# Eight attention layers on one core: where the keys' first halves stand in the queues, and which engine normalizes the first tile behind the output's product

## The chip, the core and the metric

The kernel runs on one core of a Trainium2 chip. A core has five engines with queues of their own: TensorE (PE in the profile; its weight loads are PEld), VectorE (DVE), ScalarE (ACT), GpSimd (POOL) and SyncE (SP), which here only starts DMAs. ScalarE starts DMAs too; such an instruction stands in ScalarE's queue like any other. An engine takes its instructions in order, and one that waits for another engine's result holds up all that are queued behind it. SBUF is the memory that all engines work on, PSUM the memory that TensorE writes its products to.

The metric is the device time of one execution in microseconds (us). A profiled execution also gives its span, from the first instruction to the last.

## What is computed

The reference is a Perceiver block of three stages on 512 tokens with 512 features, all in float32: a cross attention over 8192 context rows, eight layers of linear attention with a feed-forward part, and a stage of experts. The change is in the eight layers. Cut to that stage:

```python
def _block(x, p):
    Wq, bq, Wk, bk, Wv, bv, Wo, bo, ln1_s, ln1_b, Wf1, bf1, Wf2, bf2, ln2_s, ln2_b = p
    residual = x
    q = jnp.einsum('nld,da->nla', x, Wq) + bq
    k = jnp.einsum('nld,da->nla', x, Wk) + bk
    v = jnp.einsum('nld,da->nla', x, Wv) + bv
    Q = jax.nn.elu(q) + 1.0
    K = jax.nn.elu(k) + 1.0
    KV = jnp.einsum('nsh,nsh->nh', K, v)
    Ksum = jnp.sum(K, axis=1)
    Z = 1.0 / (Q * Ksum[:, None, :] + EPS_Z)
    V = Q * KV[:, None, :] * Z
    attn = jax.nn.gelu(jnp.einsum('nla,ad->nld', V, Wo) + bo)
    x = _layernorm(attn + residual, ln1_s, ln1_b)
    residual = x
    h = jax.nn.gelu(jnp.einsum('nld,df->nlf', x, Wf1) + bf1)
    ff = jax.nn.gelu(jnp.einsum('nlf,fd->nld', h, Wf2) + bf2)
    x = _layernorm(ff + residual, ln2_s, ln2_b)
    return (x, None)
```

## The kernel before, in words

**Tiles.** The 512 tokens are four tiles of 128 (t = 0 to 3), the 512 features four chunks of 128. A tensor named `cur` or `mid` has tokens on the partitions; `curT` and `midT` are the same, transposed, with features on the partitions. Weight matrices (1 MB each) come through SyncE's DMA queue into eight buffers. Six rows of biases and scales (`row`, 256 KB each) come for each layer through ScalarE's queue (L985) into nine buffers in rotation, so that a load of a coming layer waits until the last reader of an older row is done. The second and third row of layer l + 1 take the buffers of two rows that GpSimd reads at the end of layer l - 1 (L936 and L937, the affine step of the two last tiles), and ScalarE's queue has these two loads at the start of layer l. Layer 7 has no next layer to load rows for.

**Order of the work.** TensorE's order is written out by hand. For the other engines a scheduler chooses the order from the program's dependences and its own estimates; `tc.issue_after(x)` tells it that what is inside may stand in its queue only behind x.

**The features of a layer** (`features`, L638). TensorE first makes the halves of the keys for the tokens of tiles 0 and 1 (`k7.p12`), the queries' first products for the same tokens, then turns tile 2 (`turns[2]()`: four transposes into PSUM, and four copies of ScalarE into `curT`, L945), makes a third query product, turns tile 3, and makes the products of tiles 2 and 3 and then the rest of the keys by a seven-product scheme (`k7.rest`), for which sums of the two halves of the tokens are needed (`token_sums`, L719 to L722, on VectorE and GpSimd). In layer 0 the turning is `transpose_into` (L594, L595).

`k7.take` (L744) takes the first two of the keys' products out of PSUM: a copy by ScalarE (L747), an addition by VectorE (L748), and then `elu1`: L623 on VectorE, L625 and L626 on ScalarE (L626 is an exponential, with a load of the activation table ahead of it), L627 on GpSimd and L628 on VectorE. Before the change it is told to stand behind the turned copies of tile 2, and behind the last normalization of the layer before (`normed`).

**Behind the output's product** (L1063 to L1072). For each tile, TensorE multiplies by the output's weights (L1069) and `finish` (L913) adds the bias (L917, VectorE), takes the GELU (L918, ScalarE), adds the residual (L919, VectorE) and normalizes: statistics (L922, L923), an inverse square root by nine small VectorE operations (L91 to L95, L82), and the scaling. With `eng` ScalarE the scaling is two instructions, a small VectorE one (L931) and ScalarE's (L932); with `eng` VectorE it is one (L928). The scaled tile 0 is turned in the midst of tile 3's product, tiles 1, 2 and 3 later, between the products of the hidden features (`s7.p12`, L726). `turn` is four transposes (L943) and four ScalarE copies into `midT` (L945).

Of the kernel before, what the change touches and what calls it, by code (L numbers as in the profile page):

```python
# [11 lines left out]
ALU = mybir.AluOpType  # L12
# [4 lines left out]
P = 128  # L17
D = 512
DC = D // P
# [26 lines left out]
R_BO, R_S1, R_B1, R_BF2, R_S2, R_B2 = range(6)  # L46
# [8 lines left out]
def perceiver_kernel(  # L55
# [3 lines left out]
    nc = tc.nc  # L59
# [28 lines left out]
    def rsqrt_of(var, n, eps, eng=nc.vector):  # L88

        ve = small.tile([P, n], F32, tag=f"ve{n}", name="ve")  # L90
        eng.tensor_scalar(ve, var, eps, None, ALU.add)  # L91
        vh = small.tile([P, n], F32, tag=f"vh{n}", name="vh")
        eng.tensor_scalar(vh, ve, -0.5, None, ALU.mult)
        yg = small.tile([P, n], I32, tag=f"yg{n}", name="yg")
        eng.tensor_scalar(yg, ve.bitcast(I32), -0.5, float(0x5F3759DF), ALU.mult, ALU.add)  # L95
        y = yg.bitcast(F32)
        for _ in range(3):
            t = small.tile([P, n], F32, tag=f"nt{n}", name="nt")
            if n == 1:
                stt(eng, t, y, y, vh, ALU.mult, ALU.mult)  # L100
            else:
                eng.tensor_tensor(t, y, y, ALU.mult)
                eng.tensor_tensor(t, t, vh, ALU.mult)
            y2 = small.tile([P, n], F32, tag=f"ny{n}", name="ny")
            latest[0] = stt(eng, y2, t, 1.5, y, ALU.add, ALU.mult)
            y = y2
        return y
# [10 lines left out]
    def normalize(dst, src, n, eps, roots=None):  # L118
        mv, r = roots or (moments(src, n), None)
        if r is None:  # L120
            r = rsqrt_of(mv[:, :, 1], n, eps)
        for i in range(n):
            last = nc.vector.tensor_scalar(
                dst[:, i, :], src[:, i, :], mv[:, i, 0:1], r[:, i : i + 1], ALU.subtract, ALU.mult
            )
        return last
# [38 lines left out]
    behind, copied, newest = [None, None], [None], [None, None]  # L165
# [46 lines left out]
    k_sb, v_sb, xT, part, rows_of, trigs = {}, {}, {}, {}, {}, {}  # L212
# [118 lines left out]
    while min(met) < NCHUNK:  # L331
        p = k % NPAIR
# [33 lines left out]
    scores, mx, mrow, alpha, mbc, es, po = {}, {}, {}, {}, {}, {}, {}  # L366
# [158 lines left out]
    last = -1  # L525
    for u, n in enumerate(size):
# [6 lines left out]
        for i in range(n):  # L533
            d = end[u] + 1 + i * span // n // 2
            at(d, late_exponentials if d in end[-3:] else exponentials, u, i)
            last = max(d + 1, first)
# [53 lines left out]
    def transpose_into(dst, src, t, space, tag):  # L590

        pt = space.tile([P, DC, P], F32, tag=tag, name="pt")
        for dc in range(DC):
            nc.tensor.transpose(pt[:, dc, :], src[:, dc * P : (dc + 1) * P], ident)  # L594
        return nc.scalar.copy(dst[:, :, t * P : (t + 1) * P], pt)  # L595

    with ExitStack() as s_:
# [33 lines left out]
        def feature(ps, w, c0, xT, t0=0, n=T):  # L631
            for dc in range(DC):
                nc.tensor.matmul(  # L633
                    ps[:, t0 : t0 + n], w[:, dc, c0 : c0 + P], xT[:, dc, t0 : t0 + n],
                    start=(dc == 0), stop=(dc == DC - 1),
                )

        def features(k7, chunks, xT, turns, done, normed):  # L638

            held = {}

            def product(i, t0=0, n=T):
                if t0 == 0:
                    held[i] = mm.tile([P, T], F32, tag="mm", name="ps")
                feature(held[i], *chunks[i], xT, t0, n)

            if 1 in turns:
                for p in range(2):  # L650
                    k7.p12(p, 0, P, False)
                turns[1]()
                product(0, 0, P)
                for p in range(2):
                    k7.p12(p, P, P, False)
                product(0, P, P)
            else:
                for p in range(2):
                    k7.p12(p, 0, H, False)
                product(0, 0, H)  # L660
            product(1, 0, H)
            turned = turns[2]()
            with tc.issue_after(normed.ins) if normed else nullcontext():
                with tc.issue_after(turned.ins):
                    for p in range(2):
                        k7.take(p)
            product(2, 0, H)
            turned = turns[3]()
            for t in range(2):
                k7.token_sums(t)  # L670
            for t in (2, 3):
                for i in range(2):
                    product(i, t * P, P)
            product(2, H, H)

            with tc.issue_after(turned.ins):
                for i in range(3):
                    done(i, held[i], 0, T)
            k7.rest((0, 1))
            for i in range(3, len(chunks)):  # L680
                product(i)
                done(i, held[i], 0, T)
# [227 lines left out]
                    next_sums(q)  # L910
                return g0, g1

        def finish(ps, old, bias, t, eng, g=None):  # L913

            if g is None:
                g = gpool.tile([P, D], F32, tag="g", name="g")
                nc.vector.tensor_tensor(g, ps, bias, ALU.add)  # L917
            nc.scalar.activation(g, g, AF.Gelu_apprx_tanh)  # L918
            nc.vector.tensor_tensor(g, g, old[:, t, :], ALU.add)  # L919
            mv = small.tile([P, 1, 2], F32, tag="mv1", name="mv")  # L920
            st = small.tile([P, 6], F32, tag="st", name="st")
            nc.vector.bn_stats(st, g)  # L922
            nc.vector.bn_aggr(mv[:, 0, :], st)  # L923
            r = rsqrt_of(mv[:, :, 1], 1, 1e-6)
            if eng is None:
                return g, mv[:, 0, 0:1], r
            if eng is nc.vector:
                last = nc.vector.tensor_scalar(g, g, mv[:, 0, 0:1], r, ALU.subtract, ALU.mult)  # L928
            else:
                n = small.tile([P, 1], F32, tag="nmr1", name="nmr")  # L930
                last = nc.vector.scalar_tensor_tensor(n, mv[:, 0, 0:1], -1.0, r, ALU.mult, ALU.mult)  # L931
                nc.scalar.activation(g, g, AF.Identity, bias=n, scale=r)  # L932
            return g, last
# [27 lines left out]
        cur = cpl.tile([P, TT, D], F32, tag="cur", name="cur0")  # L961
        curT = cpl.tile([P, DC, T], F32, tag="curT", name="curT0")
        last = None
        for t in range(TT):
            with tc.issue_after(last.ins) if t else nullcontext():
                last = normalize(cur[:, t : t + 1], x_sb[:, t : t + 1], 1, 1e-5, rooted.get(t))
        s_.enter_context(tc.manual_schedule(engines={nc.tensor.engine}))
        transpose_into(curT, cur[:, 0, :], 0, acc, "acc")
        turns = {t: lambda dst=curT, src=cur[:, t, :], t=t: transpose_into(dst, src, t, acc, "acc") for t in (1, 2, 3)}
# [9 lines left out]
        for l in range(NL):  # L979
            w_k, w_q, w_v, w_o = ahead if l else first[0]  # L980
            w_1, w_2 = hidden_weights(l) if l else first[1]
            row = []
# [71 lines left out]
            k7 = k7 if l else keys_of_layer(w_k, curT)  # L1054
            k7.sx = [hpool.tile([P, 2, H], F32, tag="h", name="sx") for _ in range(4)]
            k7.tiles, k7.out = keys_tiles, keys_taken
            features(k7, [(w, ac * P) for w in (w_q, w_v) for ac in range(DC)], curT, turns, taken, last if l else None)


            mid = cpl.tile([P, TT, D], F32, tag="cur", name="mid")  # L1060
# [2 lines left out]
            gs = {}  # L1063
            for t in range(TT):
                po = acc.tile([P, D], F32, tag="acc", name=f"po_{l}_{t}")
                for ac in range(DC):
                    if t == TT - 1 and ac == 2:
                        turn(midT, gs[0], 0, *c1)
                    nc.tensor.matmul(  # L1069
                        po, vt[ac][:, t * P : (t + 1) * P], w_o[:, ac, :], start=(ac == 0), stop=(ac == DC - 1)  # L1070
                    )
                gs[t], last = finish(po, cur, row[R_BO], t, nc.scalar)  # L1072
            turns = {t: lambda dst=midT, g=gs[t], t=t, c=c1: turn(dst, g, t, *c) for t in (1, 2, 3)}

            hT = {}
# [52 lines left out]
            for p in range(2, NF // 2):  # L1128
# [13 lines left out]
                last = s7.p4(p)  # L1142
# [20 lines left out]
            cur = cpl.tile([P, TT, D], F32, tag="cur", name="cur")  # L1163
            if l + 1 == NL:
                break
            curT = cpl.tile([P, DC, T], F32, tag="curT", name="curT")
# [8 lines left out]
            for t in (0, 2):  # L1175
                if t:
                    ahead = attention_weights(l + 1)
                g = back.products(t, row[R_BF2], between if t else lambda q: None, next_sums(t))
# [8 lines left out]
            turns = {t: lambda dst=curT, g=gs[t], t=t, c=c2: turn(dst, g, t, *c) for t in (2, 3)}  # L1187
            k7 = made[0]
# [95 lines left out]
        for o in (4, 5):  # L1284
            w = cpl.tile([P, DC, D], F32, tag=("curT", "cur")[o % 2], name=f"f2_{o}")
# [21 lines left out]
        for q in range(1, NSQ):  # L1307
# [9 lines left out]
        po = [  # L1317
            (acc if t < 3 else mm).tile([P, D], F32, tag="acc" if t < 3 else "mm", name=f"po_f{t}")
            for t in range(TT)
        ]  # L1320
# [51 lines left out]
        for o in range(NO + 2):  # L1372
            if o < NO:
                inner(o)
            if o < 2:
                w = weights(big, f2[(6 + o) * 512 : (7 + o) * 512, :], f"f2_{6 + o}", nc.scalar)
# [79 lines left out]
```

## Time and profile before

| | us |
|---|---|
| median of 3 runs (2603.5 to 2603.98) | 2603.82 |
| profiled execution, its own time | 2604.4 |
| its span | 2602.6 |
| start of the output's product (L1069) in layers 0 and 7 | 1281.40, 2414.97 |
| TensorE busy in the span | 2513.4 |
| VectorE, ScalarE, GpSimd busy | 1746.6, 1187.6, 1413.3 |

The layers take up the span from about 1235 to 2510 us; from one layer's output product to the next it is some 162 us. A matmul of float32 shows as two passes of TensorE. The profile's groups give, for a line of the program, how long its instructions kept an engine busy, and how long the engine had been idle before them and for whom. "Idle" there is counted from the modelled end of a pass, which lies about 0.17 us behind the point at which the next pass could have started; times between starts are so much longer. The granted clock is the share of TensorE's full clock that the throttle let through.

### The profile page before, as it was taken

To read this page: it belongs to the slowest core of one execution; us is meant where nothing else is said; L and a number is where in the kernel's file an instruction comes from. 1 tells how busy PE (TensorE), PEld (TensorE's weight loads), DVE (VectorE), ACT (ScalarE), POOL (GpSimd) and SP (SyncE) were. 2 spreads that over 40 slices of the span, in tenths; PEclk is the share of its full clock that TensorE was granted. 3 is DMA by queue.
4 is the path that set the end of the run, shared out by engine and by line. 5 is a ranking of instruction groups with operands and counts; after the bars stand their busy time and mean duration, and the time that the engine had idled before them with its cause. 6 is when DMAs were issued, how large, how long until landed. Compare 5 with 4: busy or idle time off the path is not lost.

```text
span 2602.6 us, 32659 instructions
## 1 busy us (share of the span) xinstructions
PE 2513.4 (97%) x10936; PEld 1513.2 (58%) x10936; DVE 1746.6 (67%) x3762; ACT 1187.6 (46%) x2191; POOL 1413.3 (54%) x1582
## 2 busy tenths in 40 slices
PE   8999999999999999998999999999999999999998
PEld 4434333333343343333687786877868778687763
DVE  4466667767777767885666666666666766667664
ACT  2465556655566666663423415234152341524413
POOL 0255655665566666774356554565545655466512
PEclk9999999999999999998999999999999999999999
DMA  3111011111111111010522232232322323223135
GB/s 135 41 48 48 25 41 41 41 41 41 34 41 42 40 41 41 10 40 17 209 75 95 84 108 79 74 99 80 110 77 73 106 73 110 77 73 98 65 116 193
DMA packets 98376, 187.42 MB, mean 72 GB/s; under 512 B 10336, under 2 KB 10464, under 8 KB 98208
## 3 DMA queue, kind: packets, MB, share of 16 engines
q1 hardware_dynamic: 88496, 167.29, 19.9%
q10 hardware_dynamic: 8688, 15.94, 1.9%
q0 software_dynamic: 1024, 2.10, 0.2%
q8 instruction: 87, 1.43, 0.2%
q14 instruction: 81, 0.66, 0.1%
HBM read 162.22 MB, written 1.05 MB: 63 GB/s over the span
## 4 chain that ended last, share of the span: by engine, by line
PE 71%; DVE 9%; POOL 7%; issue 7%; ACT 5%; DMA 0%; ACTq 0%; SPq 0%; POOLq 0%; DVEq 0%
PE pw L726 11%; PE pb L861 9%; PE ps L633 7%; PE ps L726 7%; PE pv L259 7%; PE pk L230 6%; PE po L455 6%; PE pc L374 6%; DVE sc L434 4%; PE po L1069 4%; ACT sc L377 2%; ACT sc L435 1%; POOL es L445 1%; PE pt L218 1%; PE pf L955 1%
## 5 line engine op out<-in xcount | busy, mean ns | idle before, releaser
L445 POOL TENSOR_TENSOR es<-es,sc 128x1024 f32<-128x1024 f32 x222 | 525.1, 2365 | 114.7 <-ACT sc L435 103.7
L383 DVE TENSOR_TENSOR mx<-pc,mx 128x512 f32<-128x512 f32 x448 | 283.3, 685 | 191.7 <-ACT sc L377 191.5
L435 ACT ACTIVATE sc<-sc 128x1024 f32<-128x1024 f32 x272 | 288.1, 1063 | 243.1 <-DVE sc L434 231.9
L377 ACT COPY sc<-pc 128x512 f32<-128x512 f32 x544 | 284.1, 599 | 92.8 <-PE pc L374 77.4
L434 DVE TENSOR_TENSOR sc<-sc,mbc 128x1024 f32<-128x1024 f32 x272 | 319.4, 1209 | 3.7 <-PE mbc L411 2.2
L374 PE MATMUL pc<-qT,k 64*128 64x512 f32 x1088 | 288.1, 621 | 2.8 <-ACT v L265 1.3
L455 PE MATMUL po<-sc,v 128*64 128x512 f32 x1088 | 265.0, 608 | 0.2 <-DVE mx L383 0.2
L230 PE MATMUL pk<-xn,wkv 128*128 128x512 f32 x544 | 255.1, 613 | 7.1 <-ACT v L265 2.9
L259 PE MATMUL pv<-wkv,xn 128*128 128x512 f32 x544 | 249.6, 602 | 6.2 <-DVE sin L241 3.3
L374 PEld LDWEIGHTS pc<-qT,k 64*128 64x128 f32 x1088 | 101.1, 187 | 183.7 <-issue 78.8
L1080 ACT ACTIVATE h<-h,col 128x256 f32<-128x256 f32 x192 | 103.8, 575 | 220.7 <-DVE h L794 151.0
L230 PEld LDWEIGHTS pk<-xn,wkv 128*128 128x128 f32 x544 | 100.7, 194 | 150.1 <-issue 106.9
L918 ACT ACTIVATE g<-g 128x512 f32<-128x512 f32 x64 | 39.8, 628 | 317.2 <-DVE g L878 218.9
L259 PEld LDWEIGHTS pv<-wkv,xn 128*128 128x128 f32 x544 | 98.6, 190 | 140.5 <-issue 106.6
L726 PE MATMUL pw<-curT,cur 128*128 128x256 f32 (+1 forms) x896 | 177.2, 351 | 0.0
L713 POOL TENSOR_TENSOR cur<-w 128x256 f32<-128x256 f32 x128 | 93.3, 739 | 133.0 <-DVE g L919 83.8
L633 PE MATMUL ps<-curT,wq 128*128 128x128 f32 (+2 forms) x584 | 134.3, 391 | 27.2 <-ACT curT L945 27.0
L726 PEld LDWEIGHTS pw<-curT,cur 128*128 128x128 f32 x896 | 150.4, 191 | 16.7 <-DVE curT L719 0.2
L827 POOL TENSOR_TENSOR sh<-h 128x128 f32<-128x128 f32 x120 | 83.1, 693 | 133.3 <-PE pb L861 128.9
L455 PEld LDWEIGHTS po<-sc,v 128*64 128x64 f32 x1088 | 67.8, 137 | 145.9 <-issue 123.1
L627 POOL TENSOR_SCALAR m<-m 128x512 f32<-128x512 f32 (+1 forms) x80 | 102.0, 1287 | 75.9 <-ACT m L626 75.1
L861 PE MATMUL pb<-tw,sh 128*128 128x256 f32 x540 | 136.3, 380 | 0.0
(252 smaller groups left out, 4649.3 us busy)
## 6 DMA issues: line engine op xcount, KB each, us to landing
w<-in_wf SPq DMA_DIRECT2D x64, 1024.0 KB, 5.3
k<-cos SPq DMA_DIRECT2D x272, 64.0 KB, 2.0
cb<-in_cx SPq DMA_DIRECT2D x62, 256.0 KB, 3.6
row<-in_rows ACTq DMA_DIRECT2D x48, 256.0 KB, 4.6
f<-in_f SPq DMA_DIRECT2D x10, 1024.0 KB, 5.5
tg<-in_trig SPq DMA_DIRECT2D x16, 512.0 KB, 3.8
wk<-in_wk SPq DMA_DIRECT2D x8, 1024.0 KB, 5.2
wq<-in_wq SPq DMA_DIRECT2D x8, 1024.0 KB, 5.2
```

What stands on the lines that cost most here:

```text
L230: nc.tensor.matmul(pk, wkv[:, 0, dc, j * P : (j + 1) * P], xT[b, dc], start=(dc == 0), stop=(dc == DC - 1))
L259: nc.tensor.matmul(pv, xT[b, dc][:, t * P : (t + 1) * P], wkv[:, 1, dc, :], start=(dc == 0), stop=(dc == DC - 1))
L374: nc.tensor.matmul(pc[h], k_sb[b, p][hs, o : o + P], qT[hs, p, :], start=True, stop=True)
L377: copied[0] = nc.scalar.copy(sc[:, h, :], pc[h])
L383: behind[0] = nc.vector.tensor_tensor(mx[u][:, h, :], pc[h], mx[u][:, h, :], ALU.max)
L434: nc.vector.tensor_tensor(sc, sc, mbc[u], ALU.subtract)
L435: nc.scalar.activation(sc, sc, AF.Exp)
L445: nc.gpsimd.tensor_tensor(es[u], es[u], sc, ALU.add)
L455: nc.tensor.matmul(po[u][h * HD : (h + 1) * HD, :], v_sb[b, p][:, t * P + h * HD : t * P + (h + 1) * HD], scores[u, i][:, h, :], start=(i ...
L633: nc.tensor.matmul(ps[:, t0 : t0 + n], w[:, dc, c0 : c0 + P], xT[:, dc, t0 : t0 + n], start=(dc == 0), stop=(dc == DC - 1),)
L726: nc.tensor.matmul(ps, lhs[:, k], rhs[:, k], start=(k == 0), stop=(k == 1))
L861: nc.tensor.matmul(ps[i], lhs, rhs, start=(q == 0 and i in (1, 2, 6, 5, 4)), stop=(q == self.N - 1 and i in (1, 2, 7, 3, 4)),)
```

## The change

In `features` the two calls of `k7.take` move from behind the copies of tile 2 to behind the copies of tile 3, after the sums of the tokens in the program; the wait for the last normalization of the layer before is left out. Behind the output's product, `finish` is told to let VectorE scale tile 0 (the other tiles stay with ScalarE), and to put the residual's addition of tile 1 behind that scaling in VectorE's queue. TensorE's and SyncE's orders stay as they are. The scheduler's orders of VectorE, ScalarE and GpSimd change around the two places.

```diff
-        def features(k7, chunks, xT, turns, done, normed):
+        def features(k7, chunks, xT, turns, done):
...
-            turned = turns[2]()
-            with tc.issue_after(normed.ins) if normed else nullcontext():
-                with tc.issue_after(turned.ins):
-                    for p in range(2):
-                        k7.take(p)
+            turns[2]()
             product(2, 0, H)
             turned = turns[3]()
             for t in range(2):
                 k7.token_sums(t)
+            with tc.issue_after(turned.ins):
+                for p in range(2):
+                    k7.take(p)
...
-        def finish(ps, old, bias, t, eng, g=None):
+        def finish(ps, old, bias, t, eng, g=None, behind=None):
...
             nc.scalar.activation(g, g, AF.Gelu_apprx_tanh)
-            nc.vector.tensor_tensor(g, g, old[:, t, :], ALU.add)
+            with tc.issue_after(behind.ins) if behind else nullcontext():
+                nc.vector.tensor_tensor(g, g, old[:, t, :], ALU.add)
...
-            features(k7, [(w, ac * P) for w in (w_q, w_v) for ac in range(DC)], curT, turns, taken, last if l else None)
+            features(k7, [(w, ac * P) for w in (w_q, w_v) for ac in range(DC)], curT, turns, taken)
...
-                gs[t], last = finish(po, cur, row[R_BO], t, nc.scalar)
+
+                gs[t], last = finish(
+                    po, cur, row[R_BO], t, nc.scalar if t else nc.vector, None, last if t == 1 else None
+                )
```

## The prediction

> **What bounds the kernel now.** I read the page first, then who waited for whom on TensorE over the layers (1235 to 2510 us), then the busy time and granted clock of single stretches of 3.41 us, then the timelines of the two places that the diff touches, in the third layer (layer 2). The page, with the group of the first edit:
>
> ```profile
> PE 2513.4 (97%) x10936; PEld 1513.2 (58%) x10936; DVE 1746.6 (67%) x3762; ACT 1187.6 (46%) x2191; POOL 1413.3 (54%) x1582
> ...
> L633 PE MATMUL ps<-curT,wq 128*128 128x128 f32 (+2 forms) x584 | 134.3, 391 | 27.2 <-ACT curT L945 27.0
> ```
>
> TensorE is busy 97%: only what it waits for can be won. In the layers it has two waits that come back:
>
> ```profile
> PE ps L633 <- ACT curT L945: 27.0, 7, 4.1
> PE pt L943 <- ACT g L932: 5.5, 8, 0.7
> ```
>
> The first comes before the queries' products of the last token tile (layers 1 to 7): six of 4.1 us, and 2.42 in layer 7. The second comes before the first tile's transposes behind the output's product, 0.7 in each of eight layers. The first costs more than its idle time. Columns here: stretch, busy time of PE, PEld, DVE, ACT, POOL, granted clock, DMA:
>
> ```profile
> 1569.43:1572.85 3.42, 0.17 (x2) 0.00 (x0) 2.51 (x4) 2.72 (x5) 2.48 (x4) 1.00 0.22 77
> 1572.85:1576.26 3.41, 2.56 (x12) 2.57 (x13) 2.36 (x7) 2.29 (x7) 2.48 (x3) 0.50 0.33 77
> 1576.26:1579.68 3.42, 3.42 (x12) 2.97 (x12) 0.71 (x2) 3.04 (x6) 1.79 (x2) 0.50 0.00 0
> ...
> 2381.81:2385.22 3.41, 1.36 (x10) 1.26 (x11) 2.47 (x4) 2.82 (x8) 3.41 (x5) 1.00 0.00 0
> 2385.22:2388.63 3.41, 3.41 (x13) 2.96 (x12) 2.64 (x6) 3.32 (x6) 2.17 (x3) 0.50 0.00 0
> ```
>
> After a stretch in which TensorE was mostly idle the clock is 0.50 for the next 3.41 us or two of them. In the chain of waits the work between this wait and the pairs' products took 5.54, 6.66, 5.43, 6.57, 5.41, 6.54 and 5.47 us in layers 1 to 7; at full speed (112 ns a 128-wide pass, 216 a 256-wide one) it is 16 x 0.112 + 8 x 0.216 = 3.52. So 41.6 - 24.6 = 17.0 us are lost beside the 27.0 of idle time.
>
> **First edit: the keys' first halves behind the last tile's copies.** The timeline shows why the copies of tile 3 came late:
>
> ```profile
> 1567.07 0.38 ACT L747 COPY kf<-ps 128x256 f32<-128x256 f32 x1
> 1568.21 1.48 POOL L936 TENSOR_TENSOR cur<-g,row 128x512 f32<-128x512 f32 x1
> 1569.72 0.33 ACTq L985 DMA_DIRECT2D row<-in_rows  x1
> 1569.77 1.32 POOL L937 TENSOR_TENSOR cur<-cur,row 128x512 f32<-128x512 f32 x1
> 1570.88 1.28 ACT L626 ACT_TABLE_LOAD   x1
> 1572.26 0.33 ACTq L985 DMA_DIRECT2D row<-in_rows  x1
> 1573.20 1.48 ACT L945 ACTIVATE curT<-pt,col 128x128 f32<-128x128 f32 x4
> ```
>
> The transposes end at 1567.65 and 16 passes more keep TensorE busy to 1569.44. ScalarE has the keys' copies, activations and a table load ahead of the four copies (1573.20). The edit takes these away, but in ScalarE's new order two row loads (L985) stand between the copies of tile 2 and those of tile 3. They wait for buffers that GpSimd still reads: the first was issued at 1569.72, as L936 ended at 1569.69; the second needs L937, which ends at 1571.09. So it issues at 1571.12, takes 0.33, the copies begin at 1571.45, and the first (0.44, and 0.05 to TensorE as at 1573.64 to 1573.70) lets TensorE on at 1571.95: idle 1571.95 - 1569.44 = 2.5 us by start times in place of 4.26, 2.35 by the page's measure. Layer 7 loads no rows for a next layer, which is why its wait is 2.42 already; there nothing stays in front, and it goes.
>
> Does 2.35 us still drop the clock? The nearest row is layer 7's: 2.42 idle, 1.36 of 3.41 busy, and the clock fell for one stretch, 5.47 - 3.52 = 1.95 us. I take that: 2.35 + 1.95 = 4.3 a layer, against (27.0 - 2.4)/6 + (17.0 - 1.95)/6 = 6.6. Won: 6 x 2.3 + 4.4 (layer 7 whole) = 18.2 us. Bounds: with the clock kept in all six, 11.7 more; with two slow stretches in each (as in layers 2, 4, 6: 3.1 lost), 6.9 less. 1153.01 to 1156.42 and 1173.49 to 1176.90 (1.46 and 1.64 busy) were followed by 0.50, while 1166.66 to 1170.07 (1.83 busy) was not: the border lies near half busy, and a wait of 2.35 that a border of two stretches cuts in the middle may pass. One in four would: 2.9 us more.
>
> The Trainium skill, "TensorE: Matmul & The Clock Gate", section "Why this matters for your kernels", puts the drop at idle gaps of about 3 us and more. By that the clock would be kept in all six layers and the sum below would be 8.8 us lower (11.7 less the 2.9 counted), about 2592. Layer 7's row (2.42 us, then 0.50) disagrees, and I go by it.
>
> The moved work must fit elsewhere. ScalarE does the keys' copies and activations and the table load (0.38 + 0.35 + 1.28 + 0.5 + 0.4 + 0.5 + 0.4, 3.8 us) behind the copies, with the queries' activations behind them; VectorE's additions and POOL's L627 follow. What waits for these next is the pairs' products: they need the sums of tokens (now ahead on VectorE) and the held banks, read by L748 about 3 us before their use. At the end of the features VectorE's last L1048 waited 1.40 us for TensorE, so that chain may come 1.4 later against TensorE before it binds, and it moves forward itself with the products. I cost the move at nothing; without that cover it is up to 2.3 - 1.4 = 0.9 a layer. Layer 0 has neither row loads waiting nor these 4 us: 0 to -0.7.
>
> **Second edit: the first tile's statistics ahead of the second's addition.** Behind the output's product:
>
> ```profile
> 1614.45 0.69 DVE L919 TENSOR_TENSOR g<-g,cur 128x512 f32<-128x512 f32 x1
> ...
> 1618.85 0.66 PE L943 MATMUL pt<-ident,g 128*128 128x128 f32 x4 [0.68 <-ACT g L932]
> ...
> 1620.71 0.81 ACT L932 ACTIVATE g<-g,nmr,ny 128x512 f32<-128x512 f32 x1
> ...
> 1622.72 0.61 ACT L918 ACTIVATE g<-g 128x512 f32<-128x512 f32 x1
> ...
> 1623.78 1.50 ACT L945 ACTIVATE midT<-pt,col 128x128 f32<-128x128 f32 x4 [0.45 <-PE pt L943]
> ```
>
> Tile 0's nine small operations now run without a break from 1613.67 (about 2.0 us, as tile 3's do from 1624.82) and VectorE scales it itself (0.55): ready at 1616.2, before TensorE asks at 1618.0 (28 passes of 0.429 from 1605.99). The wait, 0.84 by start times, goes. But tile 1's addition moves from 1614.45 to 1616.2, and ScalarE's order changes too: three activations, four copies of tile 0, the activation of tile 3, then the scalings of tiles 1 and 2, three copies of tile 1, the scaling of tile 3, the fourth copy. In the old order tile 1's scaling stood ahead of tile 3's activation and tile 3's scaling behind tile 1's copies. Queue by queue: TensorE transposes (0.44), ends tile 3's product (4 x 0.43) at 1620.17 and 16 passes at 1621.96. VectorE's L917 of tile 3 (0.69, from 1620.4) is ahead of tile 1's last small operations, done near 1622.15; tile 1's scaling (0.81) lets TensorE on at 1623.07: wait 1.1. Tile 2's scaling stands before tile 1's copies and needs operations that VectorE does behind L919 and L922 of tile 3 (0.69 + 0.70): near 1624.2; copies from 1624.95, TensorE, after transposes and eight passes at 1624.4, on at 1625.45: wait 1.05. Three copies pace it (0.25 lost); tile 3's scaling (0.71 to the next start) comes before the fourth, at 1626.70: wait 0.8. Sum 3.2 us. Before, the same stretch lost 0.84 and some 0.55 in short waits for copies: 1.4. So +1.8 a layer, +14.4 in eight. Bounds: +0.5 (tile 1's chain as quick as tile 0's) to +2.6 (each step 0.25 later).
>
> These waits lie within 4.9 us, so the clock may drop here too: 1.7 us (3.41 at 0.50) where a stretch falls on the last two. Their idle time is 2.1 of 2.8 us by start times, less by the page's measure, so I take one layer in four: 3.4 us. Bounds 0 and 8 x 1.7 = 13.6.
>
> **Sum.** -18.2 + 14.4 - 2.9 + 3.4 = -3.3 on the profiled span of 2602.6 (its run 2604.4, the median of the runs 2603.82): about 2601. This is inside 0.2% (5.2 us), about what a measurement here can tell from no change. The edits cancel.
>
> **Rivals.**
> - *The clock is kept at the first place.* Then -18.2 - 11.7 + 14.4 = -15.5: 2588; from three layers of six on it is faster than 0.2%. For it: 2.35 us is just short of layer 7's 2.42. Against it: that row. With it I count a second place milder than worked out (+0.5 each: -18.2 - 2.9 + 4, 2587).
> - *The row loads don't hold the copies* (GpSimd done sooner). Up to 44 us of waiting go, less what the last chain's 1.4 us of cover caps: some 6 x 3.7 + 4.4 = 27 won, 2591 with the second edit's 14.4. Against it: L985 starting 0.03 after L936 ends.
> - *The second place drops the clock* (slower). The three waits fall together in one stretch of 3.41 us and what follows runs at 0.50, in all eight layers 13.6: -18.2 + 14.4 + 13.6 = +9.8, 2614. It decides from five or six layers on. For it: stretches with 1.36 to 1.64 busy all dropped. Against it: TensorE works between the waits.
> - That the change isn't made is excluded: every engine's order but TensorE's and SP's differs as told.
>
> **How the numbers follow.** Forecast (they cancel) 0.42, own range 2599 to 2609; the clock kept or the second place mild 0.28 and the row loads free 0.05: faster 0.33; the second place dropping the clock, or costing its upper bound, 0.25: slower. The range reaches from 2590, near the first rival, to 2612, short of the last one's end.
>
> **What would show it.** TensorE's wait for L945 of `curT` near 2.4 us in six layers and none in layer 7; L985 twice between the copies; the wait for L932 now on tile 1, about 1.0, and a new one for `midT`; the count of 0.50 stretches (ten before) near seven. Wrong if row loads issue at once, if tile 1's wait is missing, or if the clock falls at both places.

## The result, and the profile after

| | before | changed |
|---|---|---|
| median of 11 runs, us | 2603.82 | 2610.13 |
| lowest, highest | 2601.86, 2604.93 | 2608.20, 2613.53 |
| span of the profiled execution | 2602.6 | 2606.5 |

The ratio is 1.0024 with a 95% interval of 1.0015 to 1.0034: 6.3 us slower, 4 to 9 by the interval. The forecast was 2601 in a range of 2590 to 2612. The time lies inside the range, but on the other side of no change: the two edits were taken to cancel, and together they lose.

In the changed kernel's listing `L725` is the product that was L726, `L917` the GELU that was L918, and so on by one between the two edits; L943, L945, L985 and L1069 are the same. TensorE is busy 2510.0 us in place of 2513.4. The two groups of the page that answer to the one shown before and to the work behind the second edit:

```profile
L725 PE MATMUL ps<-midT,w 128*128 128x128 f32 (+1 forms) x704 | 128.8, 333 | 13.8 <-ACT midT L945 13.8
L633 PE MATMUL ps<-curT,wq 128*128 128x128 f32 (+2 forms) x584 | 127.3, 373 | 14.4 <-ACT curT L945 14.4
```

The wait of L633 went from 27.2 to 14.4, and L633 itself is busy 7 us less (134.3 before), since less of it runs at half clock. A new wait of 13.8 stands before the hidden features' products. Who waited for whom on TensorE in the layers (total, times, longest):

```profile
PE ps L633 <- ACT curT L945: 14.4, 6, 2.4
PE ps L725 <- ACT midT L945: 13.8, 15, 1.4
PE pt L943 <- ACT g L932: 8.2, 8, 1.0
PE pw L725 <- DVE kf L780: 1.6, 1, 1.6
...
PE pb L860 <- POOL sh L827: 0.6, 2, 0.3
PE po L1069 <- DVE y L1051: 0.4, 1, 0.4
```

Six waits of 2.4 in place of six of 4.1, none in layer 7: that is what the first edit was worked out to do. The wait for L932 is now that of tile 1, 1.0 in every layer. The last three lines are new and were not in the prediction's list.

Idle time alone hides the half clock and short waits. So I also added up, from the trace, how much later each TensorE pass started after the one before it than at full speed (0.112 us for a 128-wide pass, 0.216 for a 256-wide one, 0.429 for a 512-wide one; what is under some 0.03 a pass is left out). Over the eight layers, in us:

| TensorE's loss | before | changed | difference | predicted |
|---|---|---|---|---|
| tile 3's copies in the features (L633) | 44.6 | 24.5 | -20.1 | -18.2 - 2.9 = -21.1 |
| pairs' products (L725 for `kf`), L1069 for `y`, L860 in layer 6 | 0.1 | 6.4 | +6.3 | 0 |
| behind the output's product (L1069's turn, `midT`) | 12.5 | 32.2 | +19.7 | +14.4 + 3.4 = +17.8 |
| sum | | | +5.9 | -3.3 |

Of the 6.4, layers 3 and 5 have 0.98 each at `y`, layer 7 has 1.56 at `y` and 1.8 at the pairs' products, and layer 6 has 1.1 at L860. The sum agrees with the medians' 6.3; with the small overruns the first row is 24.8 after and the sum +6.3. The two spans differ by 3.9 only, because the first output product started 2.6 us earlier in the changed kernel's execution (1278.84 against 1281.40); all but the 0.4 that layer 0 gained arose ahead of the layers, where the two executions had different half-clock stretches.

The timeline of the third layer behind the output's product:

```profile
1623.33 0.15 DVE L931 SCALAR_TENSOR_TENSOR nmr<-mv,ny 128x1 f32<-128x1 f32 x1
...
1623.52 0.81 ACT L932 ACTIVATE g<-g,nmr,ny 128x512 f32<-128x512 f32 x1
...
1624.38 0.66 PE L943 MATMUL pt<-ident,g 128*128 128x128 f32 x4 [1.03 <-ACT g L932]
...
1626.01 0.81 ACT L932 ACTIVATE g<-g,nmr,ny 128x512 f32<-128x512 f32 x1 [1.68 <-DVE nmr L931]
...
1626.73 1.14 ACT L945 ACTIVATE midT<-pt,col 128x128 f32<-128x128 f32 x3
...
1627.22 1.18 PE L725 MATMUL ps<-midT,w 128*128 128x128 f32 x6 [1.29 <-ACT midT L945]
...
1627.75 0.81 ACT L932 ACTIVATE g<-g,nmr,ny 128x512 f32<-128x512 f32 x1
...
1628.96 3.36 PE L725 MATMUL ps<-midT,w 128*128 128x128 f32 x23 [0.56 <-ACT midT L945]
```

Read it by ScalarE. Tile 1's scaling (1623.52) comes when VectorE has done its last small operation (1623.33), and TensorE has waited 1.03. Tile 2's scaling (1626.01) stands in ScalarE's queue ahead of tile 1's copies, and ScalarE itself waited 1.68 for VectorE there; so the copies start at 1626.73, though TensorE had done tile 1's transposes and gone on to other products at 1624.88. Tile 3's scaling then comes before the last copy: 0.56 more. In layer 7 two of tile 1's copies come ahead of tile 2's scaling, and the loss there is 2.4 us in place of 3.8.

The chain of waits in the fourth layer shows the other loss (start, us, what):

```profile
1736.14 1.33 POOL cur L937
...
1737.49 0.33 ACTq L985
...
1737.87 0.47 ACT curT L945
...
1738.38 1.55 PE ps L633 x8
...
1771.08 0.50 DVE y L1051
...
1771.62 1.12 PE po L1069 x2
```

The first half confirms the row load: GpSimd's L937 ends, ScalarE issues the load, and only then copies. Between 1739.93 and 1771.62 TensorE is not on the chain at all: it runs over the activations on ScalarE, L627 on GpSimd and the sums on VectorE to `y`, and the output's product waits for it.

### The profile page after: what moved, and what is told of

Its sections match the earlier page's. It is cut to its first block, busy times and chain, and to the rows that moved or that the text cites. A ratio compares the mean times of both kernels' runs of the same rounds, so it can differ in the third digit from the quotient of the medians.

```text
span 2606.5 us, 32659 instructions
## 1 busy us (share of the span) xinstructions
PE 2510.0 (96%) x10936; PEld 1506.4 (58%) x10936; DVE 1749.8 (67%) x3762; ACT 1185.1 (45%) x2183; POOL 1413.4 (54%) x1582
## 3 DMA queue, kind: packets, MB, share of 16 engines
HBM read 162.22 MB, written 1.05 MB: 63 GB/s over the span
## 4 chain that ended last, share of the span: by engine, by line
PE 64%; DVE 13%; POOL 9%; issue 7%; ACT 7%; DMA 0%; SPq 0%; ACTq 0%; POOLq 0%; DVEq 0%
PE pw L725 10%; PE pb L860 9%; PE pv L259 7%; PE po L455 6%; PE pk L230 6%; PE ps L725 6%; PE pc L374 6%; PE ps L633 5%; DVE sc L434 3%; PE po L1069 2%; POOL es L445 2%; ACT sc L377 2%; ACT sc L435 1%; PE pt L218 1%; PE pf L955 1%
## 5 line engine op out<-in xcount | busy, mean ns | idle before, releaser
L917 ACT ACTIVATE g<-g 128x512 f32<-128x512 f32 x64 | 39.9, 630 | 318.0 <-DVE g L877 219.9
L725 PE MATMUL pw<-curT,cur 128*128 128x256 f32 (+1 forms) x896 | 176.2, 350 | 0.0
L725 PEld LDWEIGHTS pw<-curT,cur 128*128 128x128 f32 x896 | 149.8, 191 | 16.1
L725 PE MATMUL ps<-midT,w 128*128 128x128 f32 (+1 forms) x704 | 128.8, 333 | 13.8 <-ACT midT L945 13.8
L633 PE MATMUL ps<-curT,wq 128*128 128x128 f32 (+2 forms) x584 | 127.3, 373 | 14.4 <-ACT curT L945 14.4
L627 POOL TENSOR_SCALAR m<-m 128x512 f32<-128x512 f32 (+1 forms) x80 | 100.9, 1274 | 69.0 <-ACT m L626 64.8
```

The costliest lines, as they stand in the source:

```text
L633: nc.tensor.matmul(ps[:, t0 : t0 + n], w[:, dc, c0 : c0 + P], xT[:, dc, t0 : t0 + n], start=(dc == 0), stop=(dc == DC - 1),)
L725: nc.tensor.matmul(ps, lhs[:, k], rhs[:, k], start=(k == 0), stop=(k == 1))
```

## The experiments

Each is written against the kernel before unless it says otherwise; ratios are to the kernel before, timed beside it.

**e1_takes: the first edit alone.** 

```diff
-            turned = turns[2]()
-            with tc.issue_after(normed.ins) if normed else nullcontext():
-                with tc.issue_after(turned.ins):
-                    for p in range(2):
-                        k7.take(p)
+            turns[2]()
...
+            with tc.issue_after(turned.ins):
+                for p in range(2):
+                    k7.take(p)
```

> The first edit alone (the two takes behind tile 3's copies; finish as before). Three theories. Q, read from the changed kernel's trace: TensorE's loss at tile 3's copies falls by 20.1 us (sum of its overrun behind L633 in the features, 44.6 before, 24.5 after), but the work moved behind the copies makes the chain over ScalarE, GpSimd and VectorE to y longer than TensorE's own, which gives 6.4 back (waits at L1069 of 0.98, 0.97 and 1.55 us, 1.8 at the pairs' products and 1.1 in the back part of layer 6): 2603.8 - 13.7 = 2590. P, as the prediction had it: the move is covered, 2603.8 - 21 = 2583. X, the two edits interact (it is the second edit's delay that makes y late): without it the waits at L1069 are gone and the time is also near 2583. Q wants a wait of L1069 for y (L1051) near 1.0 in the layers whose clock stays up, P and X want none.

2590.22 us, ratio 0.9944 (0.9931 to 0.9956). TensorE's wait for tile 3's copies is 14.3 in all as in the pair, that for L932 5.5 as before, and among its waits in the layers are:

```profile
PE pw L725 <- DVE kf L780: 1.5, 1, 1.5
...
PE po L1068 <- DVE y L1050: 0.8, 2, 0.4
PE pb L860 <- POOL sh L827: 0.5, 2, 0.3
```

The three small waits are there without the second edit, so they belong to the first: Q. 13.4 us are won by the medians (14.6 by the ratio), not 21. One detail of Q fell: the loss at the output's product is not confined to layers that keep the clock. By starts, beyond the 0.85 of tile 0's turn, it was 0.99, 0.71, 0.38, 0.23, 0.03 and 0 in layers 1 to 6, though the clock dropped in layers 2 to 6, and 1.57 in layer 7.

**e2_finish: the second edit alone.**

```diff
+            with tc.issue_after(behind.ins) if behind else nullcontext():
+                nc.vector.tensor_tensor(g, g, old[:, t, :], ALU.add)
...
+                    po, cur, row[R_BO], t, nc.scalar if t else nc.vector, None, last if t == 1 else None
```

> The second edit alone (VectorE scales tile 0, tile 1's addition behind it; the takes as before). Q: TensorE's loss behind the output's product was 12.6 us over eight layers before and 32.2 in the changed kernel, so +19.6: 2623, with waits per layer near 1.0 (L932 of tile 1), 1.3 and 0.6 (midT). P, the prediction's terms: +14.4 and +3.4 for the clock, 2621.6, which is too near to be told apart by the time alone. X, interaction: the two edits alone don't add up to the pair (e1's change plus this one's differs from +6.3 by more than 3 us).

2622.19 us, ratio 1.0060 (1.0047 to 1.0073). The wait at the features is the old one (26.9, 7 times), and those behind the output's product are the pair's (13.8 for `midT`, 8.3 for tile 1's scaling). Two of the five runs took 2617.3 and three 2622.3, so 13.6 to 18.7 more than 2603.66 (the ratio makes it 15.6). With e1's -13.4 that is +0.2 to +5.3, against +6.3 for the pair, so the times alone don't exclude an interaction of 3 us. The losses by starts speak against one: at tile 3's copies 24.5 in e1 and in the pair; at the pairs' products, `y` and L860 6.7 in e1 and 6.4 in the pair; behind the output's product 30.9 here and 32.2 in the pair. In both kernels the last is 3.8 a layer (2.4 in layer 7) and 1.5 to 1.7 more, from the half clock, in few layers (two in the changed kernel, one here). The profiled run is one of the two. It lost 40.7 at tile 3's copies where the kernel before lost 44.6, since the clock dropped for one stretch a layer and never for two. What the other three did there no trace shows.

**e3_rows: the first edit, and the row loads out of the way.** Beside the first edit:

```diff
+            return turned
...
-                nc.scalar.dma_start(out=rt, in_=rows[l, i].partition_broadcast(P))
+                with tc.issue_after(copied.ins) if l > 1 and i in (1, 2) else nullcontext():
+                    nc.scalar.dma_start(out=rt, in_=rows[l, i].partition_broadcast(P))
...
-            features(k7, ...)
+            copied = features(k7, ...)
```

> The first edit, and the loads of a layer's rows 1 and 2 (layers 2 to 7) told to stand behind the layer before's copies of tile 3 in ScalarE's queue, so that they hold no copies. TensorE's wait for the copies should go in layers 1 to 6 as it did in layer 7. Q (the queues' chain from the copies to y is about as long as TensorE's work, so that it binds as soon as the wait is gone): layers 1 to 6 lose what layer 7 of the changed kernel loses, 1.8 + 1.55 = 3.4 a layer, in place of 4.64 in four and 2.98 + 0.98 in two: 6.3 less than the first edit alone, near 2584. P (the move is covered, only the row loads held it): 6 x 2.4 of waiting and 4 x 1.65 of clock go, 21 less than the first edit alone, near 2569.

2580.27 us, ratio 0.9907 (0.9893 to 0.9920): 10 less than e1, between the two but nearer to Q. The waits:

```profile
PE po L1070 <- DVE y L1052: 4.8, 14, 0.5
PE pw L726 <- DVE kf L781: 4.4, 7, 1.6
```

The wait for `curT` and every half-clock stretch of layers 1 to 7 are gone: with the takes moved, the row loads were what held the copies. But waits for `y` and for `kf` now stand in every layer from the second on, as Q said; by starts they cost some 2.7 a layer in layers 1 to 6 (2.0 at `y`, of which 0.42 before the output product's first pass, and 0.7 at the pairs' products), where Q took 3.4 from layer 7. The timeline of ScalarE behind tile 3's copies in its third layer says why:

```profile
1565.03 1.51 ACT L945 ACTIVATE curT<-pt,col 128x128 f32<-128x128 f32 x4 [0.66 <-PE pt L943]
...
1569.79 0.51 ACT L625 ACTIVATE r<-kf,col 128x256 f32<-128x256 f32 x1 [3.00 <-DVE kf L748]
```

ScalarE waits 3.00 us for the moved addition L748, which now stands behind sums of tokens on VectorE. The move put work that was done early at the head of the longest chain.

**e4_scale: only VectorE's scaling of tile 0.**

```diff
-                gs[t], last = finish(po, cur, row[R_BO], t, nc.scalar)
+                gs[t], last = finish(po, cur, row[R_BO], t, nc.scalar if t else nc.vector)
```

> Only VectorE's scaling of tile 0, without the order that puts tile 1's addition behind it. Q (the second edit's cost comes from tile 1 being made late, and from ScalarE's order that follows from it): tile 0 is ready 0.4 us earlier (0.55 on VectorE in place of 0.15 and 0.81), tile 1's addition stays where it was, so 0 to -3 us over eight layers: 2601 to 2604. P2 (VectorE's longer work is what costs: 0.4 us more of it a layer ahead of tiles 1 to 3, and ScalarE's changed order): +8 or more, 2612 or later.

2604.73 us, ratio 1.0003 (0.9994 to 1.0012): no difference that can be told, and P2 is out. The scaling by itself costs nothing that the times can tell. It wins nothing either, which Q left open: the wait before tile 0's turn shrank, and another took its place. By starts TensorE loses 0.3 us a layer more there than before, which the interval allows.

```profile
PE ps L726 <- ACT midT L945: 6.7, 8, 0.9
PE pt L943 <- DVE g L928: 1.8, 8, 0.2
```

**e5_split: e3, with the keys' copy and addition left where they were.** Beside e3's edits:

```diff
-            turns[2]()
+            turned = turns[2]()
+            with tc.issue_after(turned.ins):
+                for p in range(2):
+                    k7.take(p, False)
...
-                    k7.take(p)
+                    k7.out(2 * p, k7.o[p][0], 0, H)
...
-            def take(self, p):
+            def take(self, p, out=True):
...
-                self.out(2 * p, o0, 0, H)
+                if out:
+                    self.out(2 * p, o0, 0, H)
```

> As e3_rows (first edit, row loads behind the copies), but the take is split: ScalarE's copy and VectorE's addition of the keys' first halves stay where they were before the change, ahead of tile 3's copies (they need no table), and only the activations behind them move. Q (after the change the chain from the copies over ScalarE, GpSimd and VectorE to y binds; in e3_rows ScalarE stood idle 3.0 us after the copies, until VectorE's addition L748 came behind the token sums): the addition is done early, that idle time goes, y comes some 2 us earlier and L1070's waits for it (1.6 a layer, 11.3 in all) mostly go; but VectorE's order now has all three of the queries' L628 ahead of L781, so that the pairs' products wait some 0.5 longer. Sum -7: 2573, 2569 to 2577. Rival R (the copies L747 ahead hold tile 3's copies by 0.7, TensorE waits for them again, the clock drops): 2585 or more. Rival N (the wait at the pairs' products takes all that L1070's gives): 2580.

2566.17 us, ratio 0.9850 (0.9836 to 0.9863): 14 less than e3, twice what Q worked out, and the fastest of all. In the layers one wait that comes back is left, the second place's of the kernel before:

```profile
PE pt L947 <- ACT g L936: 5.5, 8, 0.7
```

The waits at the pairs' products, which I had expected to grow, shrank to 0.3 a layer by starts: in the third layer ScalarE's L625 started at 1563.59, as the copies ended, where e3 had waited 3.00. Another 0.6 a layer is left at `y`. This is the direct test of the step "I cost the move at nothing": the same activations moved, but with copy and addition left where they were, and 0.9 a layer is given back in place of 2.7; over the eight layers, with L860, it is 6.7 us in place of 21.2. So even the smaller move is not free.

**e6_two: the second edit, with tile 1 scaled by VectorE too.**

```diff
-                gs[t], last = finish(po, cur, row[R_BO], t, nc.scalar)
+                gs[t], last = finish(
+                    po, cur, row[R_BO], t, nc.scalar if t > 1 else nc.vector, None, last if t == 1 else None
+                )
```

> The second edit alone, but VectorE scales tile 1 as well as tile 0. ScalarE's order then has all four copies of tile 1 ahead of tile 2's scaling. Q (the second edit's waits are: 1.0 because tile 1's chain on VectorE starts late, 1.3 and 0.6 because tile 2's and tile 3's scalings stand ahead of tile 1's copies on ScalarE): the first falls to about 0.6 (0.55 on VectorE in place of 0.15 and 0.81), the other two go and leave the copies' own pace; some 2 us a layer less than e2_finish, 16 in eight: 2606. Rival V (VectorE is what is short there: 0.4 more of its time ahead of tiles 2 and 3 makes them late in turn): no better than e2_finish, 2620 or more.

2604.08 us, ratio 0.9998 (0.9989 to 1.0006): 13 to 18 less than e2's runs, all that the second edit cost. By starts the loss behind the output's product is 11.9 in place of 30.9, with 12.5 in the kernel before. The order "addition of tile 1 behind the scaling of tile 0" is still in it. TensorE's work between tile 1's transposes and the next turn is one unbroken group of 40 passes again:

```profile
1622.14 0.66 PE L944 MATMUL pt<-ident,g 128*128 128x128 f32 x4 [0.57 <-DVE g L929]
1622.63 5.77 PE L726 MATMUL ps<-midT,w 128*128 128x128 f32 x40
```

The wait before the transposes is 0.57 as expected (1.04 in e2), and the waits for `midT` are gone. So most of the second edit's cost was ScalarE's queue: tile 2's scaling, which waited for VectorE, ahead of four copies that had their data, and tile 3's ahead of the last of them.

**e7_rows_only: the kernel before, with the row loads moved as in e3.**

> The kernel before with nothing but the row loads moved behind tile 3's copies. It tells how much of the old wait of 4.1 us was the row loads'. By the trace of before: without the first load ScalarE's L625 can start when L748 is done (1568.86) in place of 1570.10, and the second load's 0.33 goes too; the table load and the activations stay ahead of the copies: the copies come 1.2 to 1.5 us earlier in six layers and the clock still drops, 7 to 9 us, and 3 more if fewer second stretches fall: 2592 to 2597. Rival K (the keys' activations alone set the old wait, the loads were hidden beside them): 2603, no change. Rival L (the loads were the larger part, the wait falls under 2 us and the clock is kept): 2580 or less.

2590.74 us, ratio 0.9945 (0.9931 to 0.9959): 13.9 won, somewhat more than worked out. The wait is 2.4 in all seven layers:

```profile
PE ps L633 <- ACT curT L946: 17.0, 7, 2.4
```

So taking away the loads wins some 1.7 of the 4.1, and taking away the keys' activations with their table load (e1) wins 1.7 as well. Either obstacle alone leaves 2.4. The two give nearly the same time, and both together (e5) give more than the sum, since only then the wait goes whole and the clock stays up; e5 also keeps copy and addition early, which e1 doesn't.

## Why the prediction was wrong

- **First edit, the wait itself: right.** 2.4 us in layers 1 to 6, none in layer 7, the loads between the copies, -20.1 against -21.1. The forecast of the clock held nearly as well: of six layers four dropped, for one stretch each, where four or five were counted. Which layers drop is a matter of where the stretches fall; in e1 it was five.
- **"I cost the move at nothing": this step failed**, and with 6.3 of the 9.2 us between -3.3 and +5.9 it is the largest part. The prediction let the chain to `y` move forward with TensorE's products, and took as cover besides that VectorE's last L1048 waited 1.40 us for TensorE in layer 2. In fact the moved work put that chain back. e1 and e7 show by how much: both leave TensorE a wait of 2.4 before tile 3's products in layers 1 to 6, and only e1 has moved the takes. The first scaling of `y` in the third layer, in e7, whose output product starts at 1600.81, and the last L1048 there (L1050 in its listing):

```profile
1596.37 0.49 DVE L1053 TENSOR_SCALAR y<-y,kvs 128x512 f32<-128x512 f32 x1 [3.76 <-POOL y L1030]
...
1601.02 0.75 DVE L1050 SCALAR_TENSOR_TENSOR kf<-ps,col,kf 128x512 f32<-128x512 f32 x1 [1.40 <-PE ps L633]
```

  and in e1, whose output product starts at 1599.80:

```profile
1598.05 0.49 DVE L1050 TENSOR_SCALAR y<-y,kvs 128x512 f32<-128x512 f32 x1 [3.77 <-POOL y L1027]
```

  `y` begins 4.44 us ahead of the output's product in e7 and 1.75 in e1, so 2.7 later; in layers 1 to 6 it is 2.1 to 2.7. Nor is the cover there in every case. In layers 2 to 7 of e7, where the clock dropped, the last L1048 waits 1.0 to 1.4, and in layer 1, which kept its clock, hardly at all:

```profile
1440.87 0.75 DVE L1050 SCALAR_TENSOR_TENSOR kf<-ps,col,kf 128x512 f32<-128x512 f32 x1 [0.17 <-PE ps L633]
```

  So in the changed kernel the move did cost next to nothing in layers 1, 2, 4 and 6 up to the output's product, where the clock still dropped. It cost 0.98 in layers 3 and 5, which kept their clock, and 3.4 in layer 7, where the whole wait went. The recorded price of 0.9 a layer comes near 0.98 by luck: 2.3 - 1.4 is what is left with the cover if the chain stays in place, and it was worked out for layers that win 2.3, which lost nothing there. e1 shows the loss without the second edit, e3 shows it in every layer from the second on, and e5 takes away two thirds of e3's by leaving copy and addition in their old place. The loss of some 1 us at L860 in layer 6 comes with the first edit too (e1, e3) and goes with e5; how it is carried there I did not follow.
- **Second edit: the mechanism right, its size a little short.** By the passes' starts in the timeline above, tile 1's late scaling cost 1624.38 - 1623.20 = 1.2 (1.1 worked out), tile 2's scaling ahead of the copies 1627.22 - 1625.78 = 1.4 (1.05), and the copies' pace with tile 3's scaling 1628.96 - 1627.89 = 1.1 (0.25 + 0.8); 1623.20, 1625.78 and 1627.89 are where the passes in front end at 0.112 each. So the term that was short is tile 2's scaling: it waited 1.68 for VectorE, until 1626.01, where the prediction's 1624.2 is 1625.45 in this kernel, whose output product starts 1.25 later. In all 3.8 a layer in place of 3.2, but only 2.4 in layer 7, which the prediction took for like the others. The clock gave 3.1 (predicted 3.4) in two layers of eight. e4 shows that VectorE's scaling alone costs nothing that can be told, and e6 that with tile 1 scaled by VectorE too the ordered addition costs nothing either: it is the two together with tiles 1 to 3 left to ScalarE. No run has the ordered addition alone.
- **The sum.** -21.1 + 17.8 was a small difference of two large terms; errors of +6.3, +1.0 and +1.9, all on the same side, turned its sign.
- **The rivals.** None of the three happened. The slower one put the loss on the clock at the second place (13.6); it was 3.1. The wait for `y` was written as a bound on a cost of nothing and should have been a rival.

What beats both kernels is e5: the activations behind the copies, copy and addition ahead, the row loads behind, and the old normalization: 2566.17, 1.5% under the kernel before.

## What to carry to other kernels

A slack that is read where the bound engine runs at half clock shrinks once an edit cures this (1.40 and 0.17 us in two layers of e7): read it in a stretch that is as fast as the edit is to make it, and ask whether the work that moves stands itself on the chain that the slack is to cover. When work is moved behind something in an in-order queue, move only the part that was in the way (here the activations with their table load) and leave the part that starts the longest chain. And look in each queue for an instruction that waits ahead of one that has its data: a DMA issue that waits for its buffer (e7) and a scaling that waits for another engine (e2 against e6) cost 14 and 13 to 18 us here.

## What was not expected of the hardware

The same wait of 2.42 us dropped the clock in one layer and not in another. Stretches of 3.41 us of the changed kernel (busy time of PE, PEld, DVE, ACT, POOL; granted clock; DMA):

```profile
1734.29:1737.70 3.41, 1.67 (x15) 1.48 (x14) 2.01 (x2) 0.00 (x0) 3.33 (x4) 1.00 0.09 34
1737.70:1741.12 3.42, 2.74 (x19) 2.54 (x20) 2.14 (x6) 3.19 (x9) 1.41 (x2) 1.00 0.38 125
1898.13:1901.54 3.41, 1.25 (x7) 1.10 (x8) 0.77 (x3) 1.76 (x6) 2.10 (x3) 1.00 0.45 126
1901.54:1904.96 3.42, 3.42 (x14) 3.15 (x14) 2.01 (x6) 3.20 (x6) 0.84 (x2) 0.50 0.09 28
```

In the fourth layer the wait is cut by the border of two stretches (1.67 and 2.74 busy) and the clock stays at 1.00; in the fifth it falls into one (1.25 busy) and the next is at 0.50. By starts the two layers lost 3.0 and 4.6 us at the copies. So a wait of this length has no fixed price here: it depends on where the stretches fall. Busy time does not decide alone near the border: 1410.02 to 1413.44 with 1.77 busy was followed by 0.50, the stretch above with 1.67 was not. The three waits at the second place (1.0, 1.3 and 0.6, with work between them) dropped the clock in two layers of eight.
